# A decoder layer in fp32: attention's order of work by fixed lags, or by a modelled clock of each engine

## The chip, the cores and the metric

The kernel runs on one core of a Trainium2 chip. The metric is device time in microseconds (us), the median of several executions. PE is the matrix engine (TensorE), PEld its weight loads, DVE the vector engine, ACT the scalar engine, POOL is GpSimd, and SP the engine that only issues DMAs here. PSUM is the matmuls' output memory, in eight banks; SBUF is the working memory.

## What is computed

The input x is 4 x 512 tokens of 512 numbers. The layer is pre-normalised: each of its three parts adds to x.

```python
x = x + attn(layernorm(x), wq, wk, wv, wo)      # 32 query heads, 8 key/value heads of 64, rope, causal softmax
x = x + xattn(layernorm(x), ctx_2048)           # both sides rounded to fp8 per block of 128, then x @ ctx.T
x = x + ffn(layernorm(x), Wg, W1, W3, W2, sw1, sw3, sw2)
# ffn: the best of 8 experts for each token, at most 256 tokens an expert, silu(x W1) * (x W3) @ W2,
#      times its softmax share, plus a shared expert of the same form; hidden size 704
```

All weights and activations are fp32, apart from the fp8-rounded ones, which travel as bf16.

## The kernel before, in words

All instructions are issued by one Python program, in the order in which it runs; each engine then executes its own instructions in that order and waits at semaphores for the others. So the program's order is each engine's queue. There are three stretches: attention with the cross product (xattn) beside it, the shared expert, and the eight routed experts.

**Attention's frame.** For each batch b of four there are 16 pairs p of query heads. A step handles four score units (a pair's 128 query rows each) in four PSUM banks tagged "sp". `steps()` lists 80 steps. The main loop goes through them, each in two half-steps: `scores` of the *next* step (L981; DVE takes the masked minimum into pm and mn, L1004; ACT the exponential, L1014), `weighted` sums of pairs that are complete (L1062), fill; then `turned` of this step (L1031, transposes of pm into the same four sp banks; ACT and DVE copy them to pT, L1042 and L1048), fill. So while DVE and ACT work at a softmax, PE has fill to do.

**Fill.** Everything else is a job: a generator that issues some instructions and yields. Positive numbers yielded are PE time (860 for a projection's k-step), negative ones ask to be left alone for so many half-steps (HALF, 7250 ns), and tuples ("dve" or "quiet", lag, us) say that the next piece is so many us of DVE work, "quiet" that no POOL work should run beside it. The jobs are: h (normalised rows, transposed), q, k, v (projections; q and k with rope, whose halves are swapped by four small DMAs on SP's queue and then added on POOL, L337 to L342), r, m, n (the softmax's sums, one over them, spread by a DMA to rrb, and multiplied in on POOL), o (output projection, L422, four token tiles), c and cs (the fp8 rounding of the context), s, t (the same of x, and the product, L627, scaled by DVE at L629 and added on POOL), w (router), and loads of weights on ACT's queue. CHAIN names the kinds whose PE work is short and follows other engines. PSUM has three more banks, tagged "mm", which jobs take in rotation, and one for the weighted sums.

**What sets the order.** `add` gives each job a half-step from which it is due, a deadline (`want`), and its predecessors, each with a lag in half-steps. `Fill.at` is a rough time: it grows by yielded PE time and by fixed sums per half-step (2700 + 2400 per weighted pair, 2100 for the turns). `Fill.gpsimd` estimates until when POOL is busy. `Fill.first` takes the first job in order of deadline that is due, whose own lag is over, and whose predecessors' lags are over; `upto` issues DVE pieces as long as a fixed room (3.2 or 4.4 us) lasts, chain pieces when they are ready, and other jobs until a share of PE time is spent. `share` spreads what remains over the half-steps. `need` forces a job out when a score needs it.

```python
        work.at += 2700 + 2400 * len(done)
        goal = min(max(goal, work.spent - 500), work.spent + 900) + share(n)
        work.upto(n, goal, 3.2, 1900, 1.35)
        turned(n, now)
        work.at += 2100
```

After attention the jobs that are left are placed between the shared expert's matmuls (`between`). Instructions, shapes and data are the same whatever the order.

## Time and profile before

| | us |
|---|---|
| median of 3 runs | 1563.94 (1563.23 to 1564.04) |
| the profiled execution | 1567.52 |
| its span, first to last instruction | 1565.7 |
| PE busy | 1530.6 |
| DVE busy | 916.7 |
| ACT busy | 543.8 |
| POOL busy | 543.1 |
| mean granted PE clock | 0.995 |

The profile's rows read like this: line, engine, operation, out<-in tiles; in a group of instructions, their busy time; in brackets or in the waits view, how long the engine had been idle before and who released it. Idle time counts only where it is on PE, which is busy in 98% of the span. [...] An fp32 matmul appears as two instructions.

### The profile page before, as it was taken

How to read it: one execution, taken by the hardware profiler on the slowest of the kernel's cores; microseconds unless marked ns; L12 is line 12 of the kernel's file. 1: busy time of each engine (PE TensorE's matmuls, PEld its weight loads, DVE VectorE, ACT ScalarE, POOL GpSimd, SP SyncE). 2: the span in 40 equal slices, each digit the busy share in tenths (PEclk: the TensorE clock that was granted, in tenths of full speed). 3: DMA queues.
4: the chain of work that ended last, by engine and by line, in shares of the span. 5: the costliest groups of instructions: out<-in, count | busy, mean ns of one | idle time of the engine just before them, and what ended most of it. 6: DMA issues, size and time to landing. Idle time of an engine off the chain costs nothing.

```text
span 1565.7 us, 22186 instructions
## 1 busy us (share of the span) xinstructions
PE 1530.6 (98%) x7329; PEld 884.2 (56%) x7329; DVE 916.7 (59%) x2714; ACT 543.8 (35%) x1627; POOL 543.1 (35%) x569
## 2 busy tenths in 40 slices
PE   9999999999999999999999999999999999999999
PEld 5455555554545544555555545455447688877864
DVE  4465843466775675977565677665556464434434
ACT  3344444433434433444443444443211221111100
POOL 2021301203334121334121331431644248776724
PEclk9999999999999999999999999999999999999999
DMA  5474430525144334524334360428142334666626
GB/s 149 128 228 137 101 102 21 149 81 136 62 101 137 93 95 123 141 68 102 92 104 115 114 163 15 115 61 258 45 148 68 108 131 162 200 208 198 214 68 215
DMA packets 118226, 193.89 MB, mean 124 GB/s; under 512 B 17120, under 2 KB 36832, under 8 KB 117600
## 3 DMA queue, kind: packets, MB, share of 16 engines
q10 hardware_dynamic: 65216, 100.42, 22.4%
q1 hardware_dynamic: 50336, 83.67, 17.7%
q0 software_dynamic: 2560, 8.39, 1.6%
q8 instruction: 58, 0.95, 0.3%
q14 instruction: 56, 0.46, 0.1%
HBM read 135.54 MB, written 27.53 MB: 104 GB/s over the span
## 4 chain that ended last, share of the span: by engine, by line
PE 85%; DVE 6%; DMA 3%; ACT 2%; issue 1%; POOL 1%; ACTq 1%; SPq 0%; DVEq 0%; POOLq 0%
PE py L422 13%; PE psq L322 11%; PE sc L981 8%; PE av L1062 8%; PE p_e L1372 8%; PE pt L1031 8%; PE p_s L1372 5%; PE epy L1289 4%; PE ys L1289 4%; PE psv L364 4%; PE psk L322 3%; PE p_s L1252 2%; DMA tsq<-t2q 2%; ACT pm L1014 1%; PE p_e L1252 1%
## 5 line engine op out<-in xcount | busy, mean ns | idle before, releaser
L1014 ACT ACTIVATE pm<-pm,mn 128x256 f32<-128x256 f32 (+3 forms) x512 | 281.0, 550 | 382.9 <-DVE mn L1004 367.2
L1004 DVE CUSTOM_DVE_ANT_0 pm<-sc,mask 128x256 f32<-128x256 f32 (+3 forms) x512 | 217.0, 485 | 98.1 <-PE sc L981 98.0
L422 PE MATMUL py<-wo,aT 128*128 128x512 f32 x512 | 241.0, 603 | 1.9 <-issue 0.8
L287 POOL TENSOR_TENSOR t1q<-t1q,tsq 128x512 f32<-128x512 f32 x64 | 82.8, 1294 | 453.3 <-DMA tsq<-t2q 209.0
L322 PE MATMUL psq<-hT,wq 128*128 128x512 f32 x512 | 237.7, 599 | 2.3 <-DVE y L629 2.2
L981 PE MATMUL sc<-kT,t1q 64*128 64x128 f32 (+3 forms) x1024 | 172.6, 455 | 10.5 <-issue 2.3
L1048 DVE COPY pT<-pt 128x128 f32<-128x128 f32 (+3 forms) x256 | 114.2, 484 | 117.1 <-PE pt L1031 108.3
L1031 PEld LDWEIGHTS pt<-ident,pm 128*128 128x128 f32 x1280 | 145.4, 141 | 35.1 <-issue 29.9
L1062 PE MATMUL av<-pT,v 128*64 128x512 f32 (+3 forms) x1024 | 154.0, 443 | 1.7 <-ACT pT L1042 1.7
L1031 PE MATMUL pt<-ident,pm 128*128 128x128 f32 x1280 | 155.3, 275 | 0.0
L1042 ACT COPY pT<-pt 128x128 f32<-128x128 f32 (+3 forms) x256 | 97.1, 431 | 153.4 <-PE pt L1031 119.3
L322 PEld LDWEIGHTS psq<-hT,wq 128*128 128x128 f32 x512 | 91.7, 190 | 102.1 <-issue 96.5
L422 PEld LDWEIGHTS py<-wo,aT 128*128 128x128 f32 x512 | 92.2, 191 | 98.0 <-issue 87.6
L981 PEld LDWEIGHTS sc<-kT,t1q 64*128 64x128 f32 x1024 | 87.0, 189 | 98.2 <-issue 63.1
L1062 PEld LDWEIGHTS av<-pT,v 128*64 128x64 f32 x1024 | 68.5, 138 | 110.8 <-issue 97.6
L287 POOL TENSOR_TENSOR acc<-acc,y 128x512 f32<-128x512 f32 x64 | 80.9, 1270 | 131.9 <-DVE y L629 130.5
L1014 ACT ACTIVATION_READ_ACCUMULATOR pm<-pm,mn 128x1 f32 x512 | 95.6, 187 | 0.0
L287 POOL TENSOR_TENSOR aT<-aT,rrb 128x512 f32<-128x512 f32 x64 | 81.5, 1305 | 15.9 <-ACT aT L1071 7.7
L430 DVE TENSOR_TENSOR acc<-py,acc 128x512 f32<-128x512 f32 x64 | 43.9, 687 | 53.3 <-PE py L422 53.0
L331 DVE TENSOR_TENSOR t2q<-psq,rt 128x512 f32<-128x512 f32 x64 | 44.0, 687 | 48.3 <-PE psq L322 46.1
L1289 PE MATMUL epy<-slot_e,slot_s 128*128 128x512 f32 x160 | 70.8, 597 | 0.0
L287 POOL TENSOR_TENSOR t1k<-t1k,tsk 128x512 f32<-128x512 f32 x16 | 20.4, 1274 | 132.2 <-DMA tsk<-t2k 64.6
(256 smaller groups left out, 2090.5 us busy)
## 6 DMA issues: line engine op xcount, KB each, us to landing
slot_e<-in_L_ffn_W_dram SPq DMA_DIRECT2D x14, 1280.0 KB
wq<-in_L_attn_wq_dram ACTq DMA_DIRECT2D x16, 1024.0 KB
tsq<-t2q SPq DMA_DIRECT2D x256, 64.0 KB
wo<-in_L_attn_wo_dram ACTq DMA_DIRECT2D x16, 1024.0 KB
rrb<-rrd ACTq DMA_DIRECT2D x32, 512.0 KB
slot_e<-in_L_ffn_W_dram SPq DMA_DIRECT2D x7, 1408.0 KB
kT<-t1k ACTq DMA_DIRECT2D x64, 128.0 KB
wk<-in_L_attn_wk_dram ACTq DMA_DIRECT2D x16, 256.0 KB
```

The source lines that it names most:

```text
L287: nc.gpsimd.tensor_tensor(*args)
L322: nc.tensor.matmul(ps, w[:, k, c0 : c0 + P], hTs[b][:, k, :], start=(k == 0), stop=(k == KC - 1),)
L422: nc.tensor.matmul(py, aT[:, r, j * P : (j + 1) * P], wts["o", a][:, r, :], start=(r == 0), stop=(r == 3),)
L981: nc.tensor.matmul(scs[g][:, o : o + nk], qTs[b, p][g * HD : (g + 1) * HD, it * P : nk], kTs[b, p // 2][g * HD : (g + 1) * HD, 0:nk], star ...
L1004: nc.vector.tensor_tensor_reduce(out=pm[:, o : o + nk], in0=scs[g][:, o : o + nk], in1=mask[:, T - nk : T], scale=-(HD**-0.5), scalar=3.0e ...
L1014: nc.scalar.activation(pm[:, o : o + nk], pm[:, o : o + nk], AF.Exp, bias=mn, scale=-1.0, accum_out=rss[b, a][:, col : col + 1],)
L1031: nc.tensor.transpose(pt[:, j * P : (j + 1) * P], pms[g][:, j * P : (j + 1) * P], ident)
L1042: nc.scalar.copy(pT[:, 0 : it + 1, it * P : nk], pt[:, o : o + nk].rearrange("p (j t) -> p j t", t=P),)
L1048: nc.vector.tensor_copy(pT[:, it + 1, 0:nk], pt[:, o : o + nk])
L1062: nc.tensor.matmul(av[g * HD : (g + 1) * HD, j * P : T], vs[b][:, j, v0 : v0 + HD], rhs, start=(j == 0), stop=(j == TB - 1),)
L1289: nc.tensor.matmul(pys[i], gT[:, c, (t + i) * P : (t + i + 1) * P], w2[:, c, :], start=False, stop=(c == HF - 1),)
L1372: nc.tensor.matmul(ps, w[:, k, :], x[:, k, :], start=k == 0, stop=k == 1)
```

## The change

The program keeps a `Clock`. `nc` is wrapped so that each instruction passes through `Clock.spend`, which notes for each engine until when it is busy, and for each piece of a tile when it is written and read, with a duration for each kind of instruction and 35 to 79 ns for an answer between engines. It also models which tile a rotating buffer replaces. The model takes full PE clock, and DMAs without contention. No instruction is added by it.

With it, lags disappear: a job is ready when the clock has what it waits for ("done", "at"), a predecessor is over when its last instruction is, and the DVE room is the time by which PE is ahead of DVE. `bank` chooses a bank itself: scores and turns have fixed ones of the four sp banks, others take the mm bank that is read soonest. Chain pieces stand back while no mm bank comes free within 150 ns. `upto` goes on filling, up to 3500 ns over its goal, while `to_turn` or `to_score` says that turns or scores aren't ready. `job_o` may be left after each of its first three token tiles. Some pieces that were "quiet" are "dve". `share` is capped by the work that is available over the next 15 half-steps, and the last group's q projections get earlier deadlines.

```diff
+class Clock:
+    ANSWER = {"tensor": 54.0, "vector": 35.0, "scalar": 35.0, "gpsimd": 79.0, "sync": 60.0}
+    def __init__(self):
+        self.free = dict.fromkeys(self.ANSWER, 0.0)
+        self.done = dict.fromkeys([*self.ANSWER, "dma"], 0.0)
+        self.born, self.log, self.rings, self.used = {}, {}, {}, {}
+        self.shape, self.count, self.pooled = None, 0, []
...
+    def wrote(self, ap):
+        return max([0.0] + [x[1] for x in self.log.get(ap.tensor.name, ()) if x[3]])
...
+    def cost(self, by, op, outs, ins, s):
+        n = max(map(self.size, (*outs, *ins)))
+        wide = [x for x in ins if self.size(x) * 2 > n]
+        psum = any(str(x.space) == "PSUM" for x in (*outs, *ins))
+        if "dma" in op:
+            if by == "gpsimd":
+                return 980.0, 4500.0
+            x = ins[0] if str(outs[0].space) == "DRAM" else outs[0]
+            ns = self.size(x) * x.ap[0][1] / 52.5
+            return 480.0, 1750.0 + ns * (2 if any(st == 0 for st, _ in ins[0].ap) else 1)
+        if by == "vector":
+            if op == "tensor_tensor_reduce":
+                return 85 + 1.04 * n, 235 + 1.04 * n
+            if op == "reciprocal":
+                d = 155 + 5.8 * n
+            elif len(wide) > 1 or psum or op in ("bn_stats", "tensor_reduce"):
+                d = 155 + 1.04 * n
+            else:
+                d = 160 + 0.52 * n
+                if n > 99:
+                    d += sum(b - s for a, b in self.pooled[-3:] if a < s < b)
+            return d - 80, d
+        if by == "scalar":
+            if op == "activation" and len(outs) > 1:
+                return 290 + 0.835 * n, 380 + 0.835 * n
+            d = (375 if len(ins) > 2 else 170 if psum else 205) + 0.83 * n
+            return d - 95, d
+        d = 187 + 2.11 * n if len(wide) > 1 else 150 + n
+        return d - 35, d
...
+    def matmul(self, op, outs, ins):
+        n, m, k = self.size(outs[0]), outs[0].ap[0][1], ins[0].ap[0][1]
+        turn, wide = op == "transpose", str(ins[0].dtype) == "dt.float32"
+        rows, cols = (P, P) if turn or k < 64 else (64 if k == 64 else P, P if m > 64 else 64 if m > 32 else 32)
+        switch = 110 + (m / 1.2 if wide else 30) if (rows, cols) != self.shape else 0.0
+        self.shape = rows, cols
+        passes = 1 if turn or not wide else 4
+        d = max(passes * n / 2.4, passes // 2 * m / 1.2, m / 1.2 if wide else 0.0) + passes
+        return switch, d * rows * cols / P**2
...
+        at, answer = 0.0, self.ANSWER[by]
+        for x, name, spot, writes in sides:
+            if writes:
+                if str(x.space) == "DRAM":
+                    continue
+                at = max(at, self.born.get(name, 0.0) + answer)
+            for other, end, who, wrote in self.log.get(name, ()):
+                if who == by and (writes or by not in ("vector", "scalar")):
+                    continue
+                if (wrote or writes) and self.meet(spot, other):
+                    at = max(at, end + answer)
+        s = max(at, self.free[by])
+        if by == "tensor":
+            switch, held = self.matmul(op, outs, ins)
+            s += switch
+            end = s + 164 + (109 if op == "transpose" else held)
+        else:
+            held, end = self.cost(by, op, outs, ins, s)
+            end += s
+        self.free[by] = s + held
+        if by == "gpsimd":
+            self.pooled.append((s, s + held))
+        who = "dma" if "dma" in op else by
+        self.done[who] = max(self.done[who], end)
...
-    nc = tc.nc
+    clock = Clock()
+    nc = Engines(clock, tc.nc)
...
-    def bank(tag, name, dt=F32):
-        bufs = {"sp": 4, "av": 1, "mm": 3}[tag]
-        return psum.tile([P, 512], dt, tag=tag, bufs=bufs, name=name)
+    PLACES = {"sp": 4, "av": 1, "mm": 3}
+    held = {}
+    def place_free(kind, i):
+        return clock.last(held[kind, i]) if (kind, i) in held else 0.0
+    def places(kind):
+        shut = [
+            (place_free(kind, i), clock.used[held[kind, i]][1] if (kind, i) in held else 0, i)
+            for i in range(PLACES[kind])
+            if not clock.used.get(held.get((kind, i)), ((kind, i) in held,))[0]
+        ]
+        return [i for *_, i in sorted(shut)]
+    def bank(kind, name, dt=F32, i=None):
+        if i is None:
+            i = places(kind)[0]
+        t = psum.tile([P, 512], dt, tag=f"{kind}{i}", name=name)
+        held[kind, i] = t.tensor.name
+        return t
+    def bank_free():
+        return min(place_free("mm", i) for i in places("mm"))
...
-    def gpsimd(us, *args):
-        nc.gpsimd.tensor_tensor(*args)
-        work.gpsimd = max(work.gpsimd, work.at) + 1000 * us
+    SOON, MARGIN = 150.0, 300.0
+    gpsimd = nc.gpsimd.tensor_tensor
...
-            yield "quiet", 0.3, 2.0
+            yield "dve", 0, 2.0
...
+        over["ps" + name] = clock.at
...
-        yield -0.6
-        gpsimd(1.27, t1, t1, ts, ALU.add)
+        yield "done"
+        gpsimd(t1, t1, ts, ALU.add)
...
+            if j < TB - 1:
+                yield "at", 0.0
...
-                yield "quiet", 0.6, 2.4
+                yield "quiet", clock.slot("bp", "qm", 2), 2.4
...
-        yield "quiet", 0, 1.0
+        yield "dve", 0, 1.0
         inv, sx = block_scales(am, ACT_EPS, KC, f"x{b}_{j}", "x")
-        yield -0.5 * pace(b)
+        yield "done"
         v = quantize_scale(h, inv, f"x{b}_{j}")
-        yield "quiet", 1 * pace(b), 2.7
+        yield "quiet", clock.slot("bp", "qm", 2), 2.7
...
-                add(za - 20, 0, ("wq", b, a), load(load_q, b, a), (before, 0.5))
+                add(za - 20, 0, ("wq", b, a), load(load_q, b, a), before)
...
-                want = 2 * r - 3.7 if a < NG - 1 or b == B - 1 else 0.8 * r + 1.1
+                want = 2 * r - 3.7 if a < NG - 1 or b == B - 1 else 0.8 * r - 4.5
...
             for i, job in enumerate(jobs):
                 if job.key[0] in CHAIN:
-                    if not room and self.at < self.cool:
+                    if not room and (at < self.cool or bank_free() > at + SOON):
                         continue
                 elif chain and job.left > 0:
                     continue
                 if (
                     job.due <= n
-                    and job.ready <= self.at
+                    and job.ready <= at
                     and (job.heavy > 0) == (room > 0)
                     and job.heavy <= room
-                    and not (job.quiet and self.gpsimd > self.at)
-                    and all(k in over and over[k] + lag * HALF <= self.at for k, lag in job.after)
+                    and not (job.quiet and clock.free["gpsimd"] > max(at, clock.free["vector"]))
+                    and all(over.get(k, 1e18) <= at for k in job.after)
                 ):
                     return jobs.pop(i)
             return None
+        def later(self, job, ready):
+            job.ready = ready
+            jobs.append(job)
+            jobs.sort(key=lambda x: x.rank())
         def step(self, job, n):
+            clock.done = dict.fromkeys(clock.done, 0.0)
             got = next(job.gen, None)
+            job.done = {k: max(x, clock.done[k]) for k, x in job.done.items()}
             if got is None:
-                over[job.key] = self.at
+                over[job.key] = job.through()
                 return None
-            if isinstance(got, tuple) or got < 0:
-                job.heavy = got[2] if isinstance(got, tuple) else 0.0
-                job.quiet = job.heavy > 0 and got[0] == "quiet"
-                job.ready = self.at + HALF * (got[1] if job.heavy else -got)
-                jobs.append(job)
-                jobs.sort(key=lambda x: x.rank())
+            if got == "done":
+                got = "at", job.through()
+            if isinstance(got, tuple):
+                job.heavy = got[2] if len(got) > 2 else 0.0
+                job.quiet = got[0] == "quiet"
+                soon = got[1] + MARGIN if got[1] else 0.0
+                self.later(job, max(soon, job.through("vector") + MARGIN if job.heavy else 0.0))
+                return None
+            job.heavy = 0.0
+            if got < 0:
+                self.later(job, clock.at - HALF * got)
                 return None
             self.spent += got
-            self.at += got
             job.left -= got
             if got and job.key[0] in CHAIN:
-                self.cool = self.at + 0.2 * HALF
+                self.cool = clock.at + 0.2 * HALF
+                if bank_free() > clock.at + SOON:
+                    self.later(job, bank_free())
...
-        def upto(self, n, pace, room=0.0, busy=0, most=9.0):
-            self.cool = max(self.cool, self.at + busy)
+        def upto(self, n, pace, slack=0.0, busy=0.0, most=9.0, until=None):
+            self.cool = max(self.cool, clock.at + busy)
+            end = max(pace, self.spent) + 3500
             while True:
-                spent, job = self.spent, self.first(n, min(room, most)) if room > 0 else None
+                spent = self.spent
+                lead = clock.at + min(max(pace - spent, 0.0), 3000.0) + slack - clock.free["vector"]
+                job = self.first(n, min(lead / 1000, most)) if lead > 0 else None
                 if job:
-                    room -= job.heavy
                     while job:
                         job = self.step(job, n)
                     if self.spent == spent:
                         continue
                 job = self.first(n, chain=True)
-                if job is None and self.spent >= pace:
+                behind = until is not None and self.spent < end and until() > clock.at + SOON
+                if job is None and self.spent >= pace and not behind:
                     return
                 while job:
                     job = self.step(job, n)
-                if self.spent < pace:
+                if self.spent < pace or behind:
...
+    def to_turn(banks):
+        pms = [pm for pms, at in banks for pm in pms]
+        return max(
+            max(clock.wrote(pm), place_free("sp", i)) - 436 * i for i, pm in enumerate(pms)
+        )
+    def to_score(ahead, done):
+        at = max(place_free("sp", i) - 430 * i for i in range(4))
+        for banks, _ in ahead:
+            for b, p, it in sum(banks, []):
+                for key, of, i in ("q", qTs, p), ("k", kTs, p // 2):
+                    if (b, i) in of:
+                        at = max(at, clock.wrote(of[b, i]))
+        return max([at] + [clock.wrote(pTs[x]) - 1900 for x in done])
...
-            scs = [bank("sp", f"sc_{n}_{c}_{g}") for g in range(2)]
+            scs = [bank("sp", f"sc_{n}_{c}_{g}", i=2 * c + g) for g in range(2)]
...
+        for m in range(n + 1, n + 16):
+            there = sum(job.left for job in todo if job.key[0] in "qkvo" and job.due + fresh(*job.key) < m)
+            most = min(most, there / (m - n))
...
+    def fresh(kind, b, i, *more):
+        if kind == "o":
+            return 4
+        first = kind == "v" or kind == "k" and i == 0 or kind == "q" and i < 4
+        return {"v": 8, "k": 2, "q": 1.5}[kind] if first and b else 0
...
-        work.at += 2700 + 2400 * len(done)
         goal = min(max(goal, work.spent - 500), work.spent + 900) + share(n)
-        work.upto(n, goal, 3.2, 1900, 1.35)
+        work.upto(n, goal, 1500.0, 0.0, 1.35, until=lambda: to_turn(now))
         turned(n, now)
-        work.at += 2100
         done = todo[d][1]
-        mid = work.spent
         goal = min(max(goal, work.spent - 500), work.spent + 900) + share(n + 1)
-        work.upto(n + 1, goal, 4.4, 900)
+        work.upto(n + 1, goal, 1500.0, 0.0, until=lambda: to_score(todo[d + 2 : d + 3], done))
...
-        work.at += ns
-        work.upto(n, 1e18, room)
+        work.upto(n, 1e18, 1000 * room - 3000)
```

In the cut parts, every `work.at` becomes `clock.at` (PE's modelled time), every lag in `add` goes, and `yield -x` in the other jobs becomes "done" or "at", as in those shown.

## The prediction

> **What bounds the kernel now.** I read the page first: TensorE (PE) is busy nearly throughout, and nothing else is near its limit.
>
> ```profile
> PE 1530.6 (98%) x7329; PEld 884.2 (56%) x7329; DVE 916.7 (59%) x2714; ACT 543.8 (35%) x1627; POOL 543.1 (35%) x569
> ```
>
> The change removes no matmul, so it can win only what PE loses between and inside its groups. The windows view says where that is (columns: us, then PE, PEld, DVE, ACT, POOL busy, PE clock, DMA).
>
> ```profile
> 20.00:1084.00 1064.00, 1039.02 (x4874) 543.05 (x4874) 684.55 (x2051) 452.88 (x1422) 274.32 (x223) 0.99 0.40 111
> 1084.00:1145.00 61.00, 59.14 (x204) 27.26 (x201) 32.10 (x83) 14.40 (x22) 30.19 (x33) 1.00 0.31 90
> 1145.00:1300.00 155.00, 151.66 (x638) 107.65 (x637) 84.08 (x221) 32.36 (x68) 66.14 (x63) 1.00 0.38 130
> 1300.00:1565.00 265.00, 262.46 (x1537) 192.84 (x1535) 108.07 (x337) 37.14 (x102) 167.75 (x230) 1.00 0.54 176
> ```
>
> Attention, 20 to 1084 us, has 1064.0 - 1039.0 = 25.0 us of plain PE idle time; the three later stretches have 1.9, 3.3 and 2.5. The waits view of PE for 20 to 1084 names the causes (waiter, who released it: us, times, longest):
>
> ```profile
> PE ptr_c L271 <- DVE qq_c L470: 4.1, 1, 4.1
> PE sc L981 <- DVE pT L1048: 2.3, 2, 1.5
> PE sc L981 <- DVE mn L1004: 2.3, 4, 0.9
> PE psq L322 <- DVE y L629: 2.2, 2, 1.5
> PE av L1062 <- ACT pT L1042: 1.7, 1, 1.7
> PE ptr_h L271 <- ACT h3T L675: 1.6, 4, 0.6
> ```
>
> They are of three kinds: scores or turns before their softmax or PSUM bank is ready, chain steps that want a bank still being read, and one accident of 4.1 us.
>
> Plain idle time is not all. A 128x512 matmul is recorded with 599 to 603 ns, yet the chain has 24 of them in 10.31 us, 430 ns each, so every gap is some 0.17 us longer than shown. Groups are also drawn out, and the clock falls after gaps. PE's timeline, at two places (start, duration, group, [idle before it]):
>
> ```profile
> 350.25 1.91 PE L1031 MATMUL pt<-ident,pm 128*128 128x128 f32 x16
> 353.66 1.71 PE L981 MATMUL sc<-kT,t1q 64*128 64x256 f32 x8 [1.50 <-DVE pT L1048]
> 355.78 2.08 PE L981 MATMUL sc<-kT,t1q 64*128 64x128 f32 x8 [0.40 <-DVE mn L1004]
> 357.78 4.40 PE L1062 MATMUL av<-pT,v 128*64 128x512 f32 x16
> ```
>
> ```profile
> 582.33 3.70 PE L322 MATMUL psq<-hT,wq 128*128 128x512 f32 x8
> 590.10 0.40 PE L271 MATMUL ptr_c<-ident_b,qq_c 128*128 128x128 bf16 x4 [4.06 <-DVE qq_c L470]
> 591.34 2.04 PE L422 MATMUL py<-wo,aT 128*128 128x512 f32 x2 [0.85 <-issue]
> 593.18 3.62 PE L1031 MATMUL pt<-ident,pm 128*128 128x128 f32 x16
> ```
>
> At 350 us the turns are followed by scores with nothing between: a half-step without filler. The weighted sums then take 4.40 us where the same group took 2.37 ten us earlier, and at 593 the turns take 3.62, not 1.91: the granted clock was 0.50 in 355.1 to 361.9, 590.6 to 597.4 and 764.7 to 768.1, 17.07 us in all, which costs about half of that, 8.5 us.
>
> To count it all I took, along PE's timeline, each group of one line and one set of shapes, and its time to the next group's start over that of the quickest quarter of its like. This estimate sums to **53 us** over attention: 29.4 at scores, turns and weighted sums; about 9.1 at the chain's transposes and its second products (L271, L627) that wait for a bank; 8.3 in the accident of 582 to 597 (4.2 of wait, the rest drawn out at the low clock); the rest small. Of the 29.4, 5.1 is the low clock of the other two stretches and 1.7 belongs to the accident, so 22.6 are waits proper. With some 8 at other fill that makes 22.6 + 9.1 + 8.3 + 5.1 + 8 = 53.
>
> **The change, part by part.**
>
> *Filling until the clock says "ready"* (to_turn, to_score, until). Now a half-step gets its share of fill and then goes on to turns or scores, ready or not. After, fill continues, by up to 3.5 us over the share, while the modelled softmax, copies or operands are more than 150 ns away. Fill comes in pieces of 860 ns, and the pieces are work that has to be done anyway, so overshoot costs nothing as long as fill is left. A wait of 1.5 us (353.66) goes; those of a few hundred ns, about as large as a clock's error, stay. I take 60% of 22.6: **13.6 us**. Bounds: 0 (the clock misses) to 20.
>
> *Banks* (fixed "sp" banks, earliest-free "mm" bank, bank_free). Scores and turns already take the four sp banks four at a time, in order, so fixing them changes no order: nothing, and no row shows a cost to hide. The mm part counts: psq waited 2.2 us for y (L629) to read a bank, transposes 1.6 and 1.1 us for copies on ACT. After, a chain step stands back until a bank is due. 70% of 9.1: **6.4 us**. Below nothing is possible only where standing back delays the chain; its queue has tens of us of slack (the next use of a turned tile is a later half-step), so the low end is 0.
>
> *The accident.* On DVE's timeline:
>
> ```profile
> 580.32 8.27 DVE L467 TENSOR_SCALAR qm_c<-qm_c 128x512 f32<-128x512 f32 x1
> 582.16 4.92 POOL L287 TENSOR_TENSOR aT<-aT,rrb 128x512 f32<-128x512 f32 x4
> 587.05 1.25 POOL L287 TENSOR_TENSOR t1k<-t1k,tsk 128x512 f32<-128x512 f32 x1
> ```
>
> A 0.4 us operation took 8.27 because POOL ran beside it. [...] The row nearest: a 128x4 tensor_scalar (iv_x, at 360.98) took 0.97 us instead of 0.17 beside a POOL addition. [...] PE pays only where the softmax is then late: 0 to 4 us, I take 2 (below). The large rounding stays quiet and against a clock that counts POOL's waits for DMAs, which the old estimate doesn't. I take 60% of 8.3: **5 us**, bounds 0 to 8 (such a collision can happen at another place).
>
> *The clock.* [...] I go by the rows: 80% of 5.1, **4 us**.
>
> *Output projection may pause per token tile* (three pauses in each of 16): an urgent q or k goes between. It adds no instruction. Behind it on ACT's queue stands the next wo load, later by the pause; it lands about 5 us after its issue, many half-steps ahead of its use. With the finer q/k deadlines it is worth part of the remaining 8: 30%, **2.4 us**, bounds -2 to 5.
>
> *Lags become modelled times.* The rope addition follows its four 64 KB hops by the modelled landing rather than 4.35 us; in the row at 590.71 to 594.81 the hop took 4.1 us, so little moves. Its POOL instruction can come a little early; then it waits at POOL's head, and behind it stand acc and aT sums. The 1 MB weight loads are let go when the last matmul that reads the slot is issued, so the issue may wait on ACT's queue with the next exponentials and pT copies behind it: at most about 1 us in each of 16, on an engine busy 453/1064 = 43%. The rrb rows (two of 512 KB) share the queues with wk or wq and then keep the DMA busy some 8 us from the issue (429.9 to 438.5), where the old lag was 10.9 us; a clock without contention lets POOL wait up to a few us at its head. Together 0 to 10 us; I take 4. With the 2 of the port, new waits are **6 us**.
>
> *After 1145 us* the same chooser only places the last chain steps: 0, bounds -2 to 2.
>
> Sum: 13.6 + 6.4 + 5 + 4 + 2.4 - 6 = **25 us**. The profiled execution would go from a span of 1565.7 to about 1540.7 and from 1567.5 to 1542.5; the median shown is 3.6 lower, 1563.9 to **1539**.
>
> **Rivals.**
>
> *Fill runs out (slower).* Fill is a fixed sum: 640 projection matmuls of 0.86 us are 550 us over 160 half-steps, 3.4 each. If "until" draws up to 3.5 us extra early on, later half-steps stand bare. A bare one is priced by 350 to 362: 1.67 + 2.19 + 2.03 = 5.9 us lost over three groups, 2.9 for a half-step that is one of two. Gains of 25 are eaten from 9 more bare half-steps on. With 15 of 160: 44 - 25 = 19 slower, **1583**. For it: the trace already has bare steps at 350 and near 1079 to 1084. Against: the new cap in share() divides what is there over the next 15 half-steps, and 3.4 us each exceeds most waits.
>
> *The stalls only move (no change).* The model drifts from the chip (no low clock, no contention), and new waits at POOL and ACT give back all: about **1563**. Against it: the engines resynchronise at each half-step, so error doesn't add up.
>
> *The clock is nearly exact.* All but 8 us go: 53 - 8 = 45, **1519**. Against: waits under 0.3 us can't be filled by 0.86 us pieces placed open-loop.
>
> *It doesn't do what it says*: pieces are ordered as before where one job alone is due, and a third of the gain shows: 8 us, **1556**.
>
> **How the numbers follow.** Forecast (1525 to 1553) 0.50; nearly exact (below 1525) 0.12; a third of it (1553 to 1561) 0.15; no change 0.07; fill runs out or another slower way 0.16. A measurement of this kernel tells about 0.2%, 3 us, from no change. So faster 0.77, same 0.07, slower 0.16. The range 1517 to 1572 leaves out the last of the exact case and the worse two thirds of the slower one.
>
> **What would show it.** Right: PE idle in attention down from 25 to about 10 us, the waits of sc and psq on pT, mn and y mostly gone from PE's list, low-clock time near zero, no DVE instruction over 3 us. Wrong: bare turns-to-scores pairs in the last third of a batch (fill ran out), new PE waits for POOL t1q or DMA (the landing model), or PE idle unchanged with new releasers (moved).

## The result: 0.84% slower, and the profile after

The changed kernel took 1576.89 us (median of 4 runs, 1574.82 to 1578.26), the kernel before 1563.62 beside it: a ratio of 1.0084, with a 95% interval of 1.0066 to 1.0101. The forecast was 1539, with a range up to 1572.

The page's first row and the windows view's attention stretch (20 to 1094 us now; attention ends 12.7 us later than before, the rest takes 2 us less):

```profile
PE 1530.8 (97%) x7326; PEld 886.6 (56%) x7329; DVE 932.2 (59%) x2714; ACT 542.8 (34%) x1625; POOL 543.9 (35%) x569
```
```profile
20.00:1094.00 1074.00, 1041.10 (x4915) 546.23 (x4916) 695.94 (x2059) 455.86 (x1425) 276.46 (x225) 0.98 0.40 111
```

Plain idle time in attention rose from 25.0 to 32.9 us (1074.0 - 1041.1). The waits view of PE for that stretch has other entries than before; every line of the program is now L194, the wrapper that feeds the clock, so one reads by tile names:

```profile
PE sc L194 <- ACT pT L194: 9.7, 5, 4.1
PE sc L194 <- POOL t1q L194: 6.8, 2, 4.1
PE py L194 <- issue: 2.9, 3, 2.5
PE py L194 <- DVE y L194: 2.3, 1, 2.3
PE psk L194 <- ACT h3T L194: 1.9, 1, 1.9
PE pt L194 <- DVE mn L194: 1.4, 2, 0.7
```

The accident (ptr_c on qq_c, 4.1) is gone. psq on y, 2.2 before, is 0.2 in the whole span. But scores now wait for copies of a turn (pT) and for a rope addition (t1q), up to 4.1 us at once. Before, one wait in attention was longer than 2 us; now there are six.

The whole account of PE, from the page and the records of the granted clock (idle is span less PE busy; the low clock, 0.50, costs half its time; the rest is PE busy less that half), in us:

| kernel | span | idle | time at the low clock in attention and the start of the tail, stretches | its cost | rest |
|---|---|---|---|---|---|
| before | 1565.7 | 35.1 | 17.1, in 3 | 8.5 | 1522.1 |
| after | 1576.5 | 45.7 | 37.5, in 9 | 18.8 | 1512.0 |

So the change did win: 10.1 us of the rest, of which the score groups account for about 7 (169.7 to 163.0 us of busy time over 1024 records, time at the low clock counted half): they are less drawn out. It lost 10.6 us in idle time, most of it in long waits, and 10.3 in the low clock beside them. The experiments ask where the long waits come from.

### The profile page after: what moved, and what is told of

Read it like the earlier page. It is cut to its first block, busy times and chain, and to the rows that moved or that the text cites. A ratio compares the mean times of both kernels' runs of the same rounds, so it can differ in the third digit from the quotient of the medians.

```text
span 1576.5 us, 22173 instructions
## 1 busy us (share of the span) xinstructions
PE 1530.8 (97%) x7326; PEld 886.6 (56%) x7329; DVE 932.2 (59%) x2714; ACT 542.8 (34%) x1625; POOL 543.9 (35%) x569
## 4 chain that ended last, share of the span: by engine, by line
PE 82%; DVE 9%; DMA 4%; ACT 2%; issue 1%; POOL 1%; SPq 0%; ACTq 0%; DVEq 0%; POOLq 0%
PE py L194 13%; PE psq L194 11%; PE p_e L194 9%; PE sc L194 9%; PE av L194 8%; PE pt L194 8%; PE p_s L194 6%; PE ys L194 5%; PE epy L194 5%; PE psk L194 3%; PE psv L194 3%; DVE pm L194 2%; DMA tsq<-t2q 1%; ACT pm L194 1%; DMA rrb<-rrd 1%
## 5 line engine op out<-in xcount | busy, mean ns | idle before, releaser
L194 ACT ACTIVATE pm<-pm,mn 128x256 f32<-128x256 f32 (+3 forms) x512 | 280.9, 550 | 359.3 <-DVE mn L194 331.4
L194 DVE CUSTOM_DVE_ANT_0 pm<-sc,mask 128x256 f32<-128x256 f32 (+3 forms) x512 | 216.9, 486 | 86.9 <-PE sc L194 86.8
L194 PE MATMUL py<-wo,aT 128*128 128x512 f32 x512 | 241.0, 600 | 5.1 <-issue 2.9
L194 PE MATMUL psq<-hT,wq 128*128 128x512 f32 x512 | 238.0, 599 | 0.2 <-DVE y L194 0.2
L194 POOL TENSOR_TENSOR t1q<-t1q,tsq 128x512 f32<-128x512 f32 x64 | 83.1, 1300 | 403.6 <-DMA tsq<-t2q 243.1
L194 DVE COPY pT<-pt 128x128 f32<-128x128 f32 (+3 forms) x256 | 115.2, 487 | 168.1 <-PE pt L194 163.7
L194 PE MATMUL sc<-kT,t1q 64*128 64x128 f32 (+3 forms) x1024 | 170.0, 462 | 18.1 <-ACT pT L194 9.7
L194 PEld LDWEIGHTS pt<-ident,pm 128*128 128x128 f32 x1280 | 145.4, 141 | 41.7 <-issue 36.3
L194 PE MATMUL av<-pT,v 128*64 128x512 f32 (+3 forms) x1024 | 157.5, 451 | 0.7 <-ACT pT L194 0.7
L194 PE MATMUL pt<-ident,pm 128*128 128x128 f32 x1280 | 155.4, 274 | 1.5 <-DVE mn L194 1.4
L194 ACT COPY pT<-pt 128x128 f32<-128x128 f32 (+3 forms) x256 | 97.6, 429 | 171.9 <-PE pt L194 144.3
L194 PEld LDWEIGHTS psq<-hT,wq 128*128 128x128 f32 x512 | 92.4, 191 | 97.1 <-issue 94.1
L194 PEld LDWEIGHTS py<-wo,aT 128*128 128x128 f32 x512 | 91.9, 190 | 97.6 <-issue 90.0
L194 PEld LDWEIGHTS sc<-kT,t1q 64*128 64x128 f32 x1024 | 87.0, 193 | 100.5 <-issue 58.5
L194 PEld LDWEIGHTS av<-pT,v 128*64 128x64 f32 x1024 | 69.9, 140 | 113.2 <-issue 103.1
L194 POOL TENSOR_TENSOR aT<-aT,rrb 128x512 f32<-128x512 f32 x64 | 81.1, 1288 | 144.8 <-DMA rrb<-rrd 51.1
L194 POOL TENSOR_TENSOR acc<-acc,y 128x512 f32<-128x512 f32 x64 | 81.4, 1275 | 87.0 <-DVE y L194 86.0
L194 ACT ACTIVATION_READ_ACCUMULATOR pm<-pm,mn 128x1 f32 x512 | 95.5, 187 | 0.0
L194 PE MATMUL ys<-slot_s,gT 128*128 128x512 f32 (+3 forms) x204 | 82.9, 589 | 2.2 <-DVE gT L194 2.2
L194 PE MATMUL p_s<-h3x,slot_s 128*128 128x256 f32 (+1 forms) x232 | 80.6, 483 | 0.0
L194 PE MATMUL epy<-slot_e,slot_s 128*128 128x512 f32 (+1 forms) x192 | 79.3, 605 | 0.0
L194 DVE TENSOR_TENSOR acc<-py,acc 128x512 f32<-128x512 f32 x64 | 43.7, 683 | 50.3 <-PE py L194 49.8
```

Of the source, the lines that this page charges most:

```text
L194: got = call(*args, **kw)
```

## Two places in the trace, and the theories

The first place is 716 to 728 us. From the timeline, VectorE, POOL and the PE group that waits (start, duration, engine, operation):

```profile
720.27 0.43 DVE L194 TENSOR_SCALAR vea<-mva 128x4 f32<-128x4 f32 x1
...
720.62 1.05 POOL L194 TENSOR_TENSOR qv_x<-h,iv_x 128x512 f32<-128x512 f32 x1
720.73 0.96 DVE L194 TENSOR_SCALAR rsa<-vea 128x4 int32<-128x4 int32 x1
...
721.62 1.28 POOL L194 TENSOR_TENSOR aT<-aT,rrb 128x512 f32<-128x512 f32 x1
721.73 1.19 DVE L194 TENSOR_SCALAR rsa<-rsa 128x4 int32<-128x4 int32 x1
...
722.83 1.31 DVE L194 TENSOR_SCALAR vea<-vea 128x4 f32<-128x4 f32 x1
722.84 1.27 POOL L194 TENSOR_TENSOR t1k<-t1k,tsk 128x512 f32<-128x512 f32 x1
...
724.06 1.28 POOL L194 TENSOR_TENSOR acc<-acc,y 128x512 f32<-128x512 f32 x1
724.17 1.18 DVE L194 TENSOR_TENSOR r0a<-vea,rsa 128x4 f32<-128x4 f32 x1
...
725.39 0.16 DVE L194 TENSOR_TENSOR r0a<-r0a,rsa 128x4 f32<-128x4 f32 x1
...
726.98 0.69 DVE L194 TENSOR_TENSOR t2q<-psq,rt 128x512 f32<-128x512 f32 x1
727.59 0.68 DVE L194 TENSOR_TENSOR t1q<-psq,rt 128x512 f32<-128x512 f32 x1
...
728.37 0.67 PE L194 MATMUL py<-wo,aT 128*128 128x512 f32 x1 [2.53 <-issue]
```

A layernorm root: operations of four columns take 0.16 us when POOL is still, as the line at 725.39, and 0.43 to 1.31 us beside POOL, each ending within 0.03 us of a POOL instruction (the first at 720.70, with POOL's aT at 720.68). Five of them cost 4.3 us more than their 0.16 each; behind them stand t2q and t1q, which read a bank of PSUM. py starts 0.1 us after t1q ends (728.27), so it seems to wait for that bank, though the trace names no releaser; PE stands for 2.53 us. Held are operations of one input (721.73, 1.19 us) as well as of two (724.17, 1.18 us); what holds them, no run here shows. The clock charges POOL's time only to single-input ones of over 99 columns, so it sees 0.16 us in every one of these.

The second place is 88 to 100 us. ACT's timeline, and the DMA view of the stretch (KB each, median us from issue to landing):

```profile
90.07 0.67 ACTq L194 DMA_DIRECT2D rrb<-rrd  x1
...
90.78 0.87 ACTq L194 DMA_DIRECT2D rrb<-rrd  x1
98.34 0.40 ACTq L194 DMA_DIRECT2D cw<-in_ctx_dram  x1
98.78 1.14 ACT L194 COPY pT<-pt 128x128 f32<-128x128 f32 x3 [7.57 <-DMA tsq<-t2q]
```
```profile
rrb<-rrd ACTq DMA_DIRECT2D x2, 512.0 KB, 6.3
...
tsq<-t2q SPq DMA_DIRECT2D x8, 64.0 KB, 6.7
```
```profile
99.48 3.85 PE L194 MATMUL sc<-kT,t1q 64*128 64x256 f32 x16 [4.14 <-ACT pT L194]
```

A hop of the rope takes 2.4 us from issue to landing as the median of the page. Here, behind two rrb loads and with 256 KB writes of xd between them, the median of eight hops is 6.7. ACT, with the issue of cw at the head of its queue, stands until the hop has landed (98.3; the two use the same semaphore, number 105, by the trace), the copies behind it come 7.57 us late, and PE waits. In the clock a hop is 1.75 us and 0.3 of wire, whatever else is in flight.

The change didn't make the hops later. By the semaphores' updates, 77 of the 317 hops that can be followed in the kernel before took over 5 us, and 44 of 320 in the changed kernel. What is new is that PE stands for them.

The clock's own list of PE starts, which the program can print, shows the blindness from the other side: after the first 35 us it holds one wait of over 1.3 us in attention, 1.6 at the score of the first batch's fourth pair. The chip shows ten over 1 us there, 23.9 in sum.

Theories: **the port** (small operations held beside POOL; the name stands for that alone), **the transfers** (late hops and ACT behind its loads), together **a blind clock**; rivals: **luck of the order** (any order has such waits somewhere), **the new rules themselves** (filling until ready, the pause) do harm.

## Experiments

Differences "to the changed kernel" are differences of the ratios to the kernel before, times 1562.5 us. Each ratio is to runs of the kernel before that ran beside it; norrb ran together with fix3, and beforenoall with hop5, not with the others of their table.

**One part undone, or one hole of the clock mended.**

quiet: roots, token scales and the cs pieces, at six places, asked for as before the change.

```diff
-            yield "dve", 0, 2.0
+            yield "quiet", 0, 2.0
```


> The changed kernel with one part undone: the score's root, the block scales and the cs pieces are asked for as quiet again, that is, taken when POOL is modelled idle, in place of dve. Port theory (small VectorE operations are held up by POOL's long ones, and the score's turn is late after them): the 38 small VectorE operations with 30 us of excess go back towards 17 with 14 us, four or five of the long TensorE waits (near 356, 391, 637, 724, 790 us) go, and the time is 1557 to 1567 us. DMA theory (q and kT are late since the engines stand at the heads of their queues for transfers): the excess falls, the waits at 99, 462 and 920 us stay, and the time is 1570 to 1577. Luck of the order: anything within 10 us of 1577, with long waits at other places.

lock: the clock charges POOL's time to all operations without a PSUM operand.

```diff
-                if n > 99:
-                    d += sum(b - s for a, b in self.pooled[-3:] if a < s < b)
+            if not psum:
+                d += sum(b - s for a, b in self.pooled[-3:] if a < s < b)
```


> The changed kernel, whose modelled clock now charges the overlap with POOL's pieces to every VectorE operation without a PSUM operand, also to those of two inputs and of under 100 elements. Port theory, in the form that the clock is wrong here and so fills too little ahead of a score: the pieces are put elsewhere, the long waits behind small VectorE operations go, 1560 to 1570 us. DMA theory: no nearer than 1572. Luck: within 10 us of 1577.

ring: in the clock a transfer of SP or ACT waits until the one eight before it has landed. The changed kernel's trace has it so, with eight semaphores in turn (cw is issued at 98.34, after the hop issued at 91.38 has landed, at 98.32). In the edit they also share one wire of 52.5 elements a ns, an assumption.

```diff
-        s = max(at, self.free[by])
+        hop = self.shared and "dma" in op and by != "gpsimd"
+        s = max(at, self.free[by], self.lanes[0] if hop else 0.0)
...
+            self.wire = max(self.wire, s + 900) + self.size(x) * x.ap[0][1] / 52.5
+            end = max(end, self.wire + 1200)
+            self.lanes = self.lanes[1:] + [end]
```


> [...] DMA theory: kT, cw and t1q are seen late in the model too, the fill ahead of their scores grows, the TensorE waits at 99, 462 and 920 us (4.1, 2.8 and 4.1 us) go with the low clock behind them, 1558 to 1568 us. Port theory: only these three go, 1568 to 1575. Luck: within 10 us of 1577.

margin330:

```diff
-    SOON, MARGIN = 150.0, 300.0
+    SOON, MARGIN = 150.0, 330.0
```


> The changed kernel with its margin for a result to be seen by TensorE at 330 ns in place of 300: a change of no weight by itself, which moves many small choices of the order. Port and DMA theories as fixed places: 1577 within 2 us, with the same long waits. Luck of the order (long waits fall where they happen to fall, and any order has some): 1567 to 1587, the long waits at other places.

| kernel | us | ratio to before | to the changed kernel |
|---|---|---|---|
| quiet | 1571.31 | 1.0057 [1.0042, 1.0071] | -4.2 us |
| lock | 1574.31 | 1.0069 [1.0047, 1.0092] | -2.3 |
| ring | 1578.15 | 1.0100 [1.0083, 1.0117] | +2.5 |
| margin330 | 1575.30 | 1.0101 [1.0084, 1.0119] | +2.7 |

Only quiet is likely more than the measurement's width, and it missed its 10 to 20 us. Both theories in their single form fell here: the wait at 728 us was still 2.25 us in quiet and 2.37 in lock, and the one at 99 us was 5.3 in ring. Luck fell as far as one small shift tests it: margin330 has the waits at 61 to 64, 102, 360, 391, 463 and 916 us again. In ring the clock did foresee the wait near 98 us (4.1 us in its list), and nothing filled it; why not stays open.

**Work left out in the order of the changed kernel.** The clock is charged as before, so the order stays the same, and only the suspected cost goes.

nohop leaves out the transfers of the rope (80 products' hops; the expectation miscounts them as 68), and adds the product itself:

```diff
-            nc.sync.dma_start(
-                out=ts[i * HH : (i + 1) * HH, :], in_=t2[o * HH : (o + 1) * HH, :]
-            )
+            clock.spend("sync", "dma_start", (), dict(out=ts[...], in_=t2[...]))
...
-        gpsimd(t1, t1, ts, ALU.add)
+        tc.nc.gpsimd.tensor_tensor(t1, t1, t2, ALU.add)
+        clock.spend("gpsimd", "tensor_tensor", (t1, t1, ts, ALU.add), {})
```


> The changed kernel in the changed kernel's own order, without the 68 rope hops: the four transfers of each product's halves are left out and POOL adds the product itself in place of its swapped halves (the rope is computed wrongly), while the modelled clock is charged as before, so that the order of work stays the same instruction for instruction. DMA theory (the clock takes a hop for a little over 3 us, and it is late behind bulk loads): the waits at 61, 99, 462 and 920 us and the low clock behind them go, 12 to 20 us: 1557 to 1565. Port theory: only the first-score wait at 61 us goes, 1570 or more, and the waits near 361, 391, 728 and 794 us stay.

noroot leaves out the Newton steps of 11 roots:

```diff
         for _ in range(3):
-            nc.vector.tensor_tensor(r0, ve, rs, ALU.mult)
+            clock.spend("vector", "tensor_tensor", (r0, ve, rs, ALU.mult), {})
...
```


> The changed kernel in its own order, without the nine small VectorE operations of the Newton steps in each of the 11 roots asked for in attention (the root is left at its first guess), the clock charged as before. Port theory: the wait at 728 us (2.5 us, and the low clock behind it) goes, with some of the smaller ones, 4 to 8 us: 1569 to 1573. If the small operations' collisions are not what TensorE waits for: 1575 to 1577.

norrb leaves out the loads that spread the reciprocal sums:

```diff
-            bulk(out=rrb[...], in_=rows[g].partition_broadcast(HD))
+            clock.spend("scalar", "dma_start", (), dict(out=rrb[...], in_=...))
...
-        gpsimd(aT, aT, rrbs[b, a][:, r, :], ALU.mult)
+        tc.nc.gpsimd.tensor_tensor(aT, aT, aT, ALU.mult)
```


> The changed kernel in its own order without the 32 loads that spread the reciprocal sums (POOL squares the weighted sums in place of scaling them), the clock charged as before. These loads stand on the same wire ahead of hops at 90 and 905 us, and POOL waits for them: if they are what makes the hops late there, the waits at 99 and 920 us go, 8 to 15 us: 1562 to 1569. If cw and the weights do it: 1573 to 1577.

nohoprrb is the three together:

> The changed kernel in its own order, without the rope hops, without the Newton steps of the roots and without the spread of the reciprocal sums to all partitions (32 loads of rrb; POOL squares the weighted sums in place of scaling them), the clock charged as before. If late transfers and held small operations together are where the clock is wrong, nearly all long waits go, and TensorE's idle time in attention falls from 30 us to about 12: 1545 to 1555. If the order itself is worse than the old one: above 1563.

The controls are the kernel before without the hops, and without all three (its edits are the same, with nothing in place of the clock's lines):

> The kernel before, without the 68 rope hops (the rope is computed wrongly), as a control: its order, with long fixed lags, has the slack to hide them. DMA theory: it gains 2 to 5 us (1559 to 1562), much less than the changed kernel gains by the same edit. If the hops cost both kernels the same, they are not what the change lost by.

> The kernel before, with the three things left out together that were left out of the changed one (rope hops, the roots' Newton steps, the loads of the reciprocal sums to all partitions), as a control: the changed order then took 1528.7 us. If the changed order is the better one once its clock is right, 1548 to 1558 here. If leaving out the work helps both alike: near 1529.

| left out | in the changed kernel | to the changed kernel | in the kernel before | to the kernel before |
|---|---|---|---|---|
| hops | 1543.23, 0.9873 [0.9844, 0.9903] | -33 us | 1560.64, 0.9987 [0.9980, 0.9993] | -2 us |
| Newton steps | 1557.25, 0.9964 [0.9953, 0.9976] | -19 | | |
| rrb loads | 1556.39, 0.9949 [0.9932, 0.9967] | -21 | | |
| all three | 1528.69, 0.9774 [0.9745, 0.9802] | -48 | 1547.46, 0.9906 [0.9889, 0.9923] | -15 |

This is the heart of it. The same hops cost the changed kernel 33 us and the old one 2. The three costs don't add up (33 + 19 + 21 = 73, against 48 measured): they work through one another. With all three gone the changed order is some 21 us faster than the old one with all three gone (0.9906 less 0.9774), so the order is a better one where what it waits for comes no later than its clock says. Roots and rrb loads weren't left out singly in the old order, so how the rest of its 15 us divides isn't known.

In nohop's waits view, attention's first entries are no longer scores:

```profile
PE pam L194 <- DVE cam L194: 2.3, 1, 2.3
PE psk L194 <- ACT h3T L194: 1.7, 1, 1.7
...
PE sc L194 <- ACT pT L194: 1.0, 3, 0.6
```

Its idle time in the span is 25.0 us (45.7), its low clock 3.4 us in one stretch (37.5 in nine). In norrb the wait at 99 us is gone, and that at 920 us, 4.15 us, is 0.78 (at 904), with the hops still there. At 920 the hops came sooner: the four issued ahead of the score landed 7.1 to 7.5 us after their issue in the changed kernel and 3.9 to 5.1 in norrb. At 99 they were still late in norrb, 4.8 to 6.1 us after their issue, with the load of cw ahead of them. What went there is ACT's standing:

```profile
90.02 0.38 ACTq L194 DMA_DIRECT2D cw<-in_ctx_dram  x1
...
93.21 0.65 ACT L194 COPY pT<-pt 128x128 f32<-128x128 f32 x2 [1.99 <-PE pt L194]
```

Without the two rrb issues ahead of it, the issue of cw is out at 90.02 and not at 98.34, and the copies run at 93.2 and not at 98.8. Nor are the rrb loads what makes hops late in general: 41 of 320 still took over 5 us in norrb.

The gain of 33 and not of my 12 to 20 comes in part from waits that I hadn't put down to the hops: those near 361, 391, 495 and 641 us went as well, and 0.75 is left of the one at 728. There POOL has fewer pieces in a row beside the root: one of its operations is held in nohop, where it was five. Over attention 13 of the roots' operations are held in nohop, against 22, so the hops bear on the port as well, but not on all of it.

noroot can't say whether the roots cost by being held or by their time on VectorE (nine operations, 0.2 us from one start to the next); the next group bears on it.

**One number of the clock, and what it does to the rest.**

hop5:

```diff
-            return 480.0, 1750.0 + ns *
+            return 480.0, 4750.0 + ns *
```


> The changed kernel with one number of its clock changed: a transfer issued by SP or ACT takes 4.75 us and its wire time in place of 1.75, so that a rope hop of 2.1 us in the model becomes 5.1, near the 5 to 7 us that the late hops took. Theory of the blind clock: with late hops foreseen, q and k are asked for and filled around, the waits at 99, 462 and 920 us go, and a third to two thirds of what leaving the hops out gave comes back: 1550 to 1565. Rival (foreseeing does not help, since no work is left to fill with, as with the ring of transfers): 1572 to 1580.

hop5quiet, as hop5 with roots and token scales "quiet":

> As the kernel with hops of 5.1 us in the clock, and with the roots and the token scales asked for as quiet again (taken when POOL is modelled idle). Blind clock: with POOL's rope additions foreseen in their later places, quiet steps again fall where POOL is idle: 3 to 8 us below the former, 1545 to 1560. If small operations beside POOL were only a by-product of the hops: equal to the former within 2 us.

| kernel | us | ratio to before | to the changed kernel |
|---|---|---|---|
| hop5 | 1585.07 | 1.0138 [1.0118, 1.0157] | +8.4 us |
| hop5quiet | 1568.02 | 1.0044 [1.0029, 1.0059] | -6.2 |

hop5 is a plain miss: foreseeing the hops made it slower. VectorE's timeline of hop5 at its longest wait shows why:

```profile
455.13 1.19 DVE L194 TENSOR_SCALAR rsa<-vea 128x4 int32<-128x4 int32 x1
456.35 1.19 DVE L194 TENSOR_SCALAR rsa<-rsa 128x4 int32<-128x4 int32 x1
457.45 1.31 DVE L194 TENSOR_SCALAR vea<-vea 128x4 f32<-128x4 f32 x1
458.80 1.18 DVE L194 TENSOR_TENSOR r0a<-vea,rsa 128x4 f32<-128x4 f32 x1
460.01 1.20 DVE L194 TENSOR_TENSOR r0a<-r0a,rsa 128x4 f32<-128x4 f32 x1
461.25 1.19 DVE L194 SCALAR_TENSOR_TENSOR rsa<-r0a,rsa 128x4 f32<-128x4 f32 x1
462.47 0.16 DVE L194 TENSOR_TENSOR r0a<-vea,rsa 128x4 f32<-128x4 f32 x1
```
```profile
PE pt L194 <- DVE mn L194: 10.9, 3, 5.5
```

The later rope additions now put a row of POOL's work beside a root: six operations held, 6.3 us more than their 0.16 each, and turns that wait 5.5 us. Asking for the roots as "quiet" moves only when they run; it takes these waits away and 14.7 us off hop5's time, where it had taken 4 off the changed kernel's. A count of the held operations goes with it (VectorE operations of up to eight columns that took over 0.3 us, and what they took beyond 0.16 each):

| kernel | held | beyond 0.16 us each |
|---|---|---|
| before | 15 | 11.1 us |
| changed | 41 | 34.0 |
| quiet | 32 | 26.5 |
| hop5 | 34 | 29.4 |
| hop5quiet | 16 | 12.5 |

So the holding costs time, and "quiet" protects only as far as the clock knows when POOL runs: with the clock's short hop it took 7.5 us of holding away, with the long one 16.9. That is how the two theories hang together. hop5 also shows that the sum isn't all: it has less holding than the changed kernel and is slower. Where the held operations fall counts too, and so do the waits for the rope, which grew as well (5.3 us at 102).

**The rules themselves.**

nountil:

```diff
-        work.upto(n, goal, 1500.0, 0.0, 1.35, until=lambda: to_turn(now))
+        work.upto(n, goal, 1500.0, 0.0, 1.35)
...
-        work.upto(n + 1, goal, 1500.0, 0.0, until=lambda: to_score(todo[d + 2 : d + 3], done))
+        work.upto(n + 1, goal, 1500.0, 0.0)
```


> The changed kernel without the added rule that the fill goes on until the clock says that the turns or scores are ready. My prediction gave the rule 13.6 us; if it is worth that in this order, 1588 to 1592. If the rule earns little because the clock is told of too few of the late results (10 us of waits modelled where the chip shows some 45): 1577 to 1583. If the rule itself does the harm: below 1574.

nopause:

```diff
-            if j < TB - 1:
-                yield "at", 0.0
```


> The changed kernel without the pause of the output projection between token tiles. My prediction gave the pause 2.4 us (bounds -2 and 5): 1579 if so. If the pause does harm, below 1573; if nothing, 1575 to 1578.

nountil took 1580.29 us, 1.0129 [1.0090, 1.0168]: the rule is worth 7 us, from nothing to 13 by the intervals. Its score records take 163.0 us too, so the 7 us that the score groups won don't come from this rule; what they come from stays open. nopause took 1603.42, 1.0267 [1.0248, 1.0286]: the pause is worth 28.6 us in this order, twelve times my figure. Without it scores stand for the copies of turns, among others at 465, 507, 519, 788 and 801 us, 3.2 to 4.7 us each:

```profile
PE sc L194 <- ACT pT L194: 27.4, 10, 4.7
PE sc L194 <- POOL t1q L194: 13.7, 3, 5.6
```

Neither rule does the harm.

**Real mends, nothing left out.**

bulksp, the bulk loads issued by SP:

```diff
-    bulk = nc.scalar.dma_start
+    bulk = nc.sync.dma_start
```


> The changed kernel with all bulk loads (weights, rows, spread sums, kT copies) issued by SP in place of ACT; the clock is charged for SP. If ACT standing at the head of its queue with a bulk load is what makes the turns late (copies to pT held 6 to 8 us near 99 and 462 us): those two waits and the low clock behind them go, 5 to 12 us: 1565 to 1572. If the hops now wait behind the bulk loads on SP instead: above 1580. If neither: 1574 to 1579.

rootpool, the Newton steps on POOL:

```diff
-            nc.vector.tensor_tensor(r0, ve, rs, ALU.mult)
-            nc.vector.tensor_tensor(r0, r0, rs, ALU.mult)
-            nc.vector.scalar_tensor_tensor(rs, r0, 1.5, rs, ALU.add, ALU.mult)
+            nc.gpsimd.tensor_tensor(r0, ve, rs, ALU.mult)
+            nc.gpsimd.tensor_tensor(r0, r0, rs, ALU.mult)
+            nc.gpsimd.tensor_scalar_add(r0, r0, 1.5)
+            nc.gpsimd.tensor_tensor(rs, r0, rs, ALU.mult)
```


> The changed kernel with the Newton steps of the roots (nine small operations on VectorE each) done by POOL as twelve. Theory that they cost by being held beside POOL: most of what leaving them out gave (19.6 us) comes back, 1560 to 1567. Theory that it is their time on VectorE: the same, since this goes too; but if POOL, the later engine for the rope, then loses what VectorE gains: 1572 to 1580.

fix2 is bulksp, rootpool and hop5 together, fix3 bulksp and rootpool:

> The changed kernel with three things mended together: hops of 5.1 us in the clock, bulk loads issued by SP, Newton steps of the roots on POOL. Theory of the blind clock: below the kernel with the long hops and quiet roots (1568) and below the kernel before (1562): 1548 to 1560. Rival, that a longer hop in the clock does no good by itself (1585 when alone): 1563 to 1575.

> The changed kernel with bulk loads issued by SP and the Newton steps of the roots on POOL, and the clock's own time for a transfer. If the two mends add up (9 and 13 us): 1553 to 1557, below the version with long hops (1558.7), and the long hop is of no use. If the long hop is what made that version the best: 1562 to 1568.

| kernel | us | ratio to before | to the changed kernel |
|---|---|---|---|
| bulksp | 1568.09 | 1.0045 [1.0027, 1.0063] | -6.1 us |
| rootpool | 1563.79 | 1.0010 [1.0002, 1.0019] | -11.6 |
| fix3 | 1570.92 | 1.0048 [1.0031, 1.0065] | -5.6 |
| fix2 | 1558.67 | 0.9975 [0.9959, 0.9991] | -17.0 |

bulksp came as expected at 99 and 462 us, where the scores' waits for ACT's copies are gone; waits for rope additions at 66 and 908 us are left, and one of 3.79 us at 33 us is new, where four copies of kT now stand ahead of the hops on SP's queue (the first hops are issued at 27.91 us; 22.74 in the changed kernel):

```profile
PE sc L194 <- POOL t1q L194: 11.6, 4, 3.8
PE sc L194 <- DVE pT L194: 7.5, 4, 2.0
```

rootpool landed in its range. fix3 missed: the two mends together gave no more than bulksp alone, with waits of 4.9 and 5.3 us for rope additions at 906 and 1045 us. With the longer hop in the clock as well (fix2) both are gone, though a wait of 6.1 us for ACT's copy of v at 781 us is new, and the kernel is faster than the one before, by 0.25% [0.09, 0.41]. So the longer hop does harm alone (+8.4 us) and good here (11.4 us from fix3 to fix2).

## Why the prediction was wrong, step by step

*What bounds the kernel, and the 53 us to be had.* Not shown as a size. With the three costs left out, PE is idle for 16.0 us in the span and the time is 35 us below the kernel before, but the old order gets 15 of these by the same cuts.

*Filling until the clock says "ready", 13.6.* Right in sign, mis-sized: 7 us, poorly resolved. The drawn-out score groups did get shorter by about 7 us, but they are as short without the rule.

*Banks, 6.4, and the accident, 5.* The waits they named are gone (psq on y 2.2 to 0.2, qq_c 4.1 to nothing), and no VectorE instruction is over 1.64 us now (8.27 before). But py waits 2.3 us for y at 391 us and 2.5 at 728, so waits for a bank came up at other places. Neither was tried alone.

*The clock, 4.* Failed: 17.1 us at the low clock became 37.5. That 80% of 5.1 us would go, no run shows. The rows on which it stood held in the main: all six waits over 2 us in attention, and two of the four between 1 and 2, have a stretch of 3.4 or 6.8 us beside them (the shortest is 1.11 us at 359.3, before the stretch at 361.1), so the new waits were paid nearly twice, 10.6 us of idle and 10.3 of clock. It isn't a rule: those at 495 and 641 us, 1.1 us each, have none, nor has one of 2.97 us in bulksp (66.5).

*Output projection may pause, 2.4.* Sign right, size wrong: 28.6 us in this order.

*Lags become modelled times, 4, and the port, 2, together 6 us of new waits.* **This is the step that failed.** I priced the hop by one row, 4.1 us from the first of four issues to the addition, and wrote that little moves. In the changed kernel the same took 9.4 us at 910 to 919, and it had taken 9.0 in the kernel before, with the rrb loads ahead, in the stretch that I read for these loads:

```profile
431.52 2.49 SPq L337 DMA_DIRECT2D tsk<-t2k  x4
...
440.50 1.29 POOL L287 TENSOR_TENSOR t1k<-t1k,tsk 128x512 f32<-128x512 f32 x1 [9.51 <-DMA tsk<-t2k]
```

Of POOL waiting for rrb and of the port I took a few us, as costs that stand side by side. No run shows the 2 us of the port as a cost of its own; the traces show held VectorE time, 23 us more over the span than before (34.0 less 11.1).

The three causes cost 48 us in the changed kernel and 15 in the old one, so the change brought some 34 us of them, where I had 6. By subtraction the 13 us lost are a gain of 21, which the order shows with the three left out, less this loss of 34; I had a gain of 31. What the causes cost through other parts of the change is counted with the loss.

What I missed is the room in the old order. The rope's own lag of 4.35 us didn't cover the late hops (the addition at 440.50 waited at POOL's head), yet PE hardly stood for them (beforenohop gains 2 us). So the room lay in the other lags and deadlines; in which of them wasn't tried. And I argued against "the stalls only move" that the engines resynchronise at each half-step. That doesn't help at the step where a score's operand is late: PE stood for 4.14 and 4.15 us at 99 and 920 us.

*Rivals.* None is what happened. "The stalls only move" had the mechanism, a clock without contention, and the time of no change. "Fill runs out" had the sign, but the long waits are for late operands.

*Signs.* "New PE waits for POOL t1q" was named as a sign of being wrong, and came. PE idle in attention, to fall to about 10 us, rose to 32.9, and the time at the low clock, to go to near zero, doubled. The sign that no VectorE instruction is over 3 us came, since the accident is gone.

Open: why the fill left a foreseen wait in ring, what the rrb loads cost beyond the waits at 99 and 920 us, and the shares of the new banks and of the cap in share(), which weren't tried.

## What to carry to other kernels

A planner that replaces fixed lags by a modelled clock loses the slack for everything the model doesn't know; before removing a lag, look in the old trace for the slowest transfer and the most delayed small operation that it hides, not the median one. Mending one hole of such a model can cost more than it gives (hop5), because the other holes decide what falls on what; test the holes by leaving the work out with the order kept, in the old order too. And a wait of 2 to 4 us on TensorE mostly counts nearly double here, since in the changed kernel each of them in attention had a stretch of 3.4 or 6.8 us at the low clock, 0.50, beside it (10.6 us of idle time more than before, 10.3 of clock).

## What the chip showed that I had not expected

Four-column operations on VectorE, 0.16 us, took 1.18 to 1.31 us each beside POOL, six in a row (hop5, 455 to 462 us). A 64 KB hop between partitions took 2.4 us as a median and 6.7 beside two 512 KB loads and 256 KB writes, with ACT's copies held 7.57 us behind the issue of a third load (changed kernel, 88 to 100 us).
